# First FFN: block outputs stored by block, gathered by token in the attention stage; block list from six batches

## The chip, the core and the metric

The kernel runs on one core of one Trainium2 chip. The metric is device time in microseconds (us) of one launch; below it is the median over several runs. Engines: PE (TensorE, matrix products), DVE (VectorE), ACT (ScalarE), POOL (GpSimd) and SP (SyncE, which here only starts plain DMAs). POOL starts the indirect DMAs, whose row numbers come from a table in SBUF.

## The reference

One macaron block on x of 8 batches x 1024 tokens x 256 features, in f32:

```python
x = x + 0.5 * ffn(layernorm(x))
x = x + linear_attention(layernorm(x))
x = x + 0.5 * ffn(layernorm(x))
```

`ffn` is a mixture of 16 experts with two chosen per token, plus a shared expert for every token:

```python
weights, idx = gate(xf)              # softmax scores, 2 of 4 groups kept, then the top 2 experts
combine = (one_hot(idx, E) * weights[..., None]).sum(1)
h = silu(einsum(xf, We1) + be1) * (einsum(xf, We3) + be3)
y = einsum(combine, einsum(h, We2) + be2)
z = silu(xf @ ws1 + bs1) * (xf @ ws3 + bs3) @ ws2 + bs2
return y + z
```

The linear attention has 16 heads of 16 features: relu on queries and keys, a sum of keys and a context matrix per head over all 1024 tokens of a batch, a division by the key sum, and an output projection with bias.

## The kernel before

**Sizes.** T = 8192 tokens; a token's row has D = 256 floats. Rows are handled in blocks of RB = 256, on 128 partitions x 2. A batch is 8 tiles of 128 tokens. With two experts per token there are 16384 routed rows in each FFN.

**Four kinds of stage, in order.**

1. *Routing, 0 to about 250 us.* Round by round (`for r in range(B + 1)`), for each batch: layer norm and transposes (`normed`), the gate and the row numbers (`route`, a chain of small steps on PE and DVE), and the shared expert of an earlier batch (`shared_units`). `route` ends with 16 indirect DMAs on POOL per batch (L467) that scatter the batch's normalised rows to the table `xs_d`, sorted by expert. A row there is 264 floats: 256 of data, then the row number of the output and the gate weight, which an iota (L456) and a small product (L461) on POOL put there, for each of the two choices.
2. *Blocks of the first FFN, about 250 to 530 us.* A block is 256 rows of one expert ("whole"), or two half blocks of 128 rows of any experts ("pair"). Which rows a block takes is read from lists made on the chip. The list of whole blocks is made by `first_map` from the counts after seven of the eight batches, so that blocks can run while the last batch is routed: N1 = 40 whole blocks. The rest, N2 = 64 half blocks, is listed by `second_map` once all eight are counted. 69 blocks (`USUAL`) always run; three more stand under a condition and run only if the counts need them (here they don't).
3. *Linear attention, about 530 to 1004 us*, in 10 rounds: round r begins batch r (`begin`: take up the first FFN's outputs with `combine`, layer norm, transposes), runs the attention of batch r-1, and finishes batch r-2 (`finish`: layer norm and routing for the second FFN).
4. *Blocks of the second FFN* and a tail with the shared expert's units and the output, to the end.

**One block.** `rows` (L654 whole, L660 pair) loads the rows from `xs_d` into a buffer `xg` (4 buffers) through SP's queue. `weights` (L672) copies the expert's weights. `transpose` turns the rows on PE (L678, into `pxg`), ACT copies them out (L683, `xgT`), and DVE copies the two extra columns into `at` (L686, L687; 6 buffers). `first` is the first product on PE (L699), with silu on ACT (L705) and the gate product on DVE (L706, `hb`). `second` is the second product on PE (L725, `qy`); DVE adds the bias (a copy of which, `b2c`, L723, it made) and multiplies by the gate weight (L731, one instruction per 128 rows, `yo`), and POOL scatters each 128 rows by token to `ys_d` (L736), two indirect DMAs a block.

The order of the blocks' instructions is written by hand: in iteration i come the row load of block i+4, the weights of i+2, the transposes of i+1, the first product of i, the second product of i-2, and one step of the side work (`behind`: the last batch's routing, the second list, and DMAs that fill the ends of the experts' tables).

**Taking up the outputs.** In `combine`, SP loads a batch's two output rows per token from `ys_d` in eight plain DMAs of 256 KB (L855), and DVE adds each to x (L856, 128x512). In `attention`, DVE adds the projection's bias (L867, `bpj`); PE makes keys and queries (L877, `pk`) and their sums (L885, `pgs`); DVE makes `dg` (L896), from which PE spreads the key sums (L901); then come the context, the projection (L946, L954, `pp`) and the sum into x.

Each engine takes its instructions in the order of the program. In all stages but the blocks, a scheduler sets that order.

Of the kernel before, what the change touches and what calls it, by code (L numbers as in the profile page):

```python
# [11 lines left out]
I32 = mybir.dt.int32  # L12
# [14 lines left out]
def macaron_kernel(  # L27
# [36 lines left out]
    CAP = T + P  # L64
    DR = D + 8
    SKIP = 1 << 24
# [4 lines left out]
    N1 = ((T - N) * K - E * (RB - 1)) // RB // VL * VL  # L71

    N2 = -(-((K * T - E) // P + E - NR * N1) // VL) * VL
    NBLK = N1 + N2 // NR
    NBH = -(-max(N1, N2 + 1) // VL) * VL
# [20 lines left out]

    xs_d = tc.dram_tile([E * CAP + RB, DR], F32, name="xs_d")
    xs_views = dram_disjoint_views(xs_d, B * NT * K + E + 2)
# [70 lines left out]
    iblk = ramp(NBH, 0, 1, "iblk")  # L169
    gm1 = ramp(NG, -1, 1, "gm1")  # L170
# [6 lines left out]
    headmask = const.tile([P, P // HD, HD], F32, name="headmask")  # L177
# [136 lines left out]
    def route(base, which, b, xns, xnT, fine=False):  # L314

        name = f"{which}_{b}"

# [13 lines left out]
        for nb in range(NB):  # L331
# [25 lines left out]
        hi = rp.tile([P, npair], F32, tag="hi", name=f"hi_{name}")  # L357
        lo = rp.tile([P, npair], F32, tag="lo", name=f"lo_{name}")
        nc.vector.tensor_tensor(hi[:], pairs[:, :, 0], pairs[:, :, 1], ALU.max)
        nc.vector.tensor_tensor(lo[:], pairs[:, :, 0], pairs[:, :, 1], ALU.min)  # L360
# [3 lines left out]
        g2 = rp.tile([P, NT * NG], F32, tag="g2", name=f"g2_{name}")  # L364
        l2 = rp.tile([P, NT * NG], F32, tag="l2", name=f"l2_{name}")
        gsv = gs.rearrange("p j g -> p (j g)")
        nc.vector.tensor_tensor(l2[:], lv[:, :, 0], lv[:, :, 1], ALU.max)
        nc.vector.tensor_tensor(g2[:], hv[:, :, 0], hv[:, :, 1], ALU.min)
        nc.vector.tensor_tensor(g2[:], g2[:], l2[:], ALU.max)
        nc.vector.tensor_tensor(gsv, hv[:, :, 0], hv[:, :, 1], ALU.max)  # L370
        nc.vector.tensor_tensor(gsv, gsv, g2[:], ALU.add)
# [10 lines left out]
        won = rp.tile([P, NT, NG], F32, tag="won", name=f"won_{name}")  # L382
        lost = rp.tile([P, NT, NG], F32, tag="lost", name=f"lost_{name}")
        nc.vector.tensor_reduce(lost[:], cg.rearrange("p j a g -> p j g a"), axis=AX.X, op=ALU.add)
        nc.vector.tensor_reduce(won[:], cg[:], axis=AX.X, op=ALU.add)
        nc.vector.tensor_tensor(lost[:], lost[:], won[:], ALU.subtract)
        nc.vector.tensor_tensor(
            lost[:], lost[:], gm1[:].unsqueeze(1).to_broadcast([P, NT, NG]), ALU.is_ge
# [57 lines left out]
        row = rp.tile([P, NT, K], F32, tag="row", name=f"row_{name}")  # L446
        nc.vector.tensor_reduce(row[:], tmp[:], axis=AX.X, op=ALU.add)
        rowi = rp.tile([P, NT, K], I32, tag="rowi", name=f"rowi_{name}", bufs=2)
        nc.vector.tensor_copy(rowi[:], row[:])
# [30 lines left out]
    def counts(base, name, unit):  # L480

        cnt = rp.tile([1, E], F32, tag="cnt", name=f"cnt_{name}", bufs=2)
        nc.vector.tensor_tensor(cnt[:], base[0:1, :], eoff[0:1, :], ALU.subtract)
        nc.vector.tensor_scalar(cnt[:], cnt[:], 1.0 / unit, None, ALU.mult)
        return cnt

    def whole(cnt, name, op):

        more = half("xn", [1, E, MB], f"more_{name}")
        nc.vector.tensor_tensor(  # L490
            more[:], cnt[:].unsqueeze(2).to_broadcast([1, E, MB]),
            iblk[0:1, 0:MB].unsqueeze(1).to_broadcast([1, E, MB]), op,
        )
        nblk = rp.tile([1, E], F32, tag="nb", name=f"nb_{name}")
        nc.vector.tensor_reduce(nblk[:], more[:], axis=AX.X, op=ALU.add)
        return nblk

    def listed(nblk, off, name, res, unit):
# [35 lines left out]
        if off is not None:  # L534

            nc.vector.tensor_copy(rv[:, N2 : N2 + 1], end[:, E - 1 : E])
# [8 lines left out]
    def first_map(base, which):  # L545


        name = f"{which}a"
        cnt = counts(base, name, RB)
        nc.vector.tensor_scalar(cnt[:], cnt[:], -1.0, None, ALU.add)  # L550
        nblk = whole(cnt, name, ALU.is_ge)
        maps = []
        for _ in listed(nblk, None, name, maps, RB):
            pass
        end = rp.tile([1, E], F32, tag="done", name=f"done_{name}", bufs=2)
        nc.vector.tensor_tensor_scan(end[:], ones[0:1, 0:E], nblk[:], 0.0, ALU.mult, ALU.add)
        nc.vector.tensor_tensor(end[:], end[:], nblk[:], ALU.subtract)
        nc.vector.tensor_scalar(end[:], end[:], -1.0, float(N1), ALU.mult, ALU.add)
        nc.vector.tensor_scalar(end[:], end[:], 0.0, None, ALU.max)
        nc.vector.tensor_tensor(end[:], end[:], nblk[:], ALU.min)  # L560
        nc.vector.tensor_scalar(end[:], end[:], float(NR), None, ALU.mult)

        fill = half("xn", [P, DR], f"fill_{which}")
        nc.gpsimd.memset(fill[:], 0.0)
        nc.gpsimd.memset(fill[:, D : D + 1], float(SKIP))
        return maps, end, fill

    def second_map(base, which, maps, done):
# [7 lines left out]
        yield from listed(nblk, done, name, maps, P)  # L576

    def fill_up(last, fill):

        v = xs_views[B * NT * K + E]  # L580
        nc.sync.dma_start(out=v[E * CAP : E * CAP + P, :], in_=fill[:])
        for e in range(E):
# [11 lines left out]
    def behind(routing, base, which, maps, done, fill):  # L594

        for _ in range(7):
            next(routing)
            yield
# [3 lines left out]
        fills = fill_up(last, fill)  # L602
# [9 lines left out]
    def blocks(maps, which, steps, between, tail):  # L612
# [9 lines left out]
        b2 = biases(which)  # L622

# [25 lines left out]
        def rows(i):  # L649
            xg[i] = mid.tile([P, NR, DR], F32, tag="u1", name=f"xg_{which}_{i}", bufs=4)  # L650
# [23 lines left out]
        def transpose(i):  # L674
# [8 lines left out]
            nc.scalar.copy(xgT[i][:], pt[:])  # L683

# [26 lines left out]
        def second(i):  # L711
            py = ps_y.tile([P, NR, D], F32, tag="y", name=f"qy_{which}_{i}")
            yo = mid.tile([P, NR, D], F32, tag="u3", name=f"yo_{which}_{i}", bufs=4)
            h, a = hh.pop(i), at.pop(i)
            w2s = [wall[:, bass.ds(e, 1), W2 : W2 + D] for e in evals[i]]
            b2c = []
# [133 lines left out]
    def combine(which, b, xt):  # L850

        for j in range(0, NT, 2):
            for k in range(K):
                y = mid.tile([P, 2, D], F32, tag="u1", name=f"y_{which}_{b}_{j}_{k}", bufs=4)
                nc.sync.dma_start(out=y[:], in_=ys_v[k, b, :, j : j + 2, :])  # L855
                nc.vector.tensor_tensor(  # L856
                    xt[:, j : j + 2, :], xt[:, j : j + 2, :], y[:], ALU.add
                )
            yield
# [101 lines left out]
    def part(gen, n):  # L961

        for _ in range(n):
            next(gen, None)
            yield
# [11 lines left out]
    def normed(which, b):  # L977
# [3 lines left out]
        yield from layernorm(xs[b], f"f{which}_{b}", xns[b], DR, parts)  # L981
# [5 lines left out]
    for r in range(B + 1):  # L987
# [6 lines left out]
        if r >= 1:  # L994
            routing = route(base, 0, r - 1, xns.pop(r - 1), xnTs[r - 1], r == B)
        if r == B:
            maps, done, fill = first_map(base, 0)
            steps = behind(routing, base, 0, maps, done, fill)
        if r == B - 1:
            run(routing)  # L1000
        run(
            normed(0, r) if r < B else None,
            routing if r < B else part(routing, 2),
# [43 lines left out]
    def begin(b):  # L1047
        yield from combine(0, b, xs[b])
# [67 lines left out]
    def first_half():  # L1116
# [10 lines left out]
        maps, 1, behind(routing, base, 1, maps, done, fill), by_block(moves), first_half  # L1127
# [136 lines left out]
```

## Time and profile before

| | us |
|---|---|
| median of 6 runs (1388.65 to 1399.74) | 1391.33 |
| the profiled execution | 1383.5 |
| its span | 1381.8 |
| first block's transposes of the first FFN | 250.15 |
| its last block matmul ends | 521.46 |
| first load of block outputs | 530.14 |
| `dg` of batch 0 | 581.89 |
| first block of the second FFN | 1004.8 |
| tail | 1266 to 1381.8 |

The times in a trace are microseconds from the start of the span. The clock is the share of full speed that TensorE was granted, 0.941 in the mean. A line of a window gives the busy time (and instruction count) of PE, PE's weight loads, DVE, ACT and POOL in it, then the granted clock, the DMA engines' busy share, and GB/s. A line of a timeline gives start, duration, engine, line, operation and operands, shapes and count, and in brackets the idle time ahead with what ended it. `A <- B: 64.4, 24, 5.9` among the waits says that A waited for B for 64.4 us in all, 24 times, 5.9 us at most.

### The profile page before, as it was taken

Reading aid. Unit: us, or ns where it says so; the run is one execution under the profiler, and the core shown is the slowest. Engines: PE = TensorE matmul, PEld = TensorE weight load, DVE = VectorE, ACT = ScalarE, POOL = GpSimd, SP = SyncE. Lnnn points to the kernel's source line nnn. Section 1 sums busy time; section 2 is a strip of 40 time slices with the busy share of each in tenths; the row PEclk is TensorE's granted clock in tenths of the full one; section 3 lists DMA queues with packets and bytes.
Section 4 is the critical chain, followed back from the end, with each engine's and each line's share of the span. In section 5 each row is a group of like instructions: output and inputs, shape, how many; then the busy total and the mean of one; then the engine's idle time right before and its main releaser. Section 6 shows DMA issues by size and latency. Waiting matters only on the chain. (4 is left out here: it accounts for less than half of the span.)

```text
span 1381.8 us, 20671 instructions
## 1 busy us (share of the span) xinstructions
PE 1190.5 (86%) x5728; PEld 852.9 (62%) x5728; DVE 883.9 (64%) x2878; ACT 541.0 (39%) x1120; POOL 581.5 (42%) x719
## 2 busy tenths in 40 slices
PE   7898877688789997899878879899997889899997
PEld 3455444576678884566545546555576678786554
DVE  6786547566456566768648548637686545565587
ACT  6555422222225451554544544542432223453110
POOL 1566556265565552002252252350536666565010
PEclk9999999899899999999889889999998899999999
DMA  9334323455565534622362330110435555552996
GB/s 358 133 124 151 121 102 109 156 178 187 179 187 165 163 122 146 217 106 106 126 207 93 131 124 24 41 63 1 155 113 175 175 175 180 151 169 88 324 370 249
DMA packets 96102, 212.20 MB, mean 154 GB/s; under 512 B 17382, under 2 KB 45291, under 8 KB 92273
## 3 DMA queue, kind: packets, MB, share of 16 engines
q1 hardware_dynamic: 68288, 134.77, 30.4%
q0 software_dynamic: 27696, 76.07, 14.9%
q8 instruction: 49, 0.80, 0.3%
q14 instruction: 69, 0.56, 0.1%
HBM read 110.75 MB, written 102.64 MB: 154 GB/s over the span
## 5 line engine op out<-in xcount | busy, mean ns | idle before, releaser
L736 POOL DMA_INDIRECT ys_d<-yo,at x276 | 276.4, 1001 | 239.0 <-DVE rest L731 173.9
L699 PE MATMUL q<-xgT,wc 128*128 128x128 f32 (+1 forms) x1568 | 290.2, 335 | 60.1 <-ACT xgT L683 32.4
L467 POOL DMA_INDIRECT xs_d<-xn_f,rowi x256 | 263.9, 1031 | 111.3 <-issue 61.1
L699 PEld LDWEIGHTS q<-xgT,wc 128*128 128x128 f32 x1568 | 236.3, 199 | 88.3 <-ACT xgT L683 41.0
L683 ACT COPY xgT<-pxg 128x512 f32<-128x512 f32 x138 | 81.4, 590 | 281.9 <-PE pxg L678 94.1
L796 PE MATMUL p_s<-xnT_f,ws_sb 128*128 128x512 f32 x352 | 163.7, 604 | 1.1 <-ACT hs_s L800 0.9
L731 DVE CUSTOM_DVE_ANT_0 yo<-qy,b2c,at 128x256 f32<-128x256 f32 x276 | 122.8, 482 | 61.7 <-remote 19.1
L706 DVE SCALAR_TENSOR_TENSOR hb<-q,wc,hb 128x128 f32<-128x128 f32 (+1 forms) x196 | 73.5, 400 | 133.5 <-PE q L699 64.4
L815 PE MATMUL py_s<-ws_sb,hs_s 128*128 128x256 f32 x512 | 133.6, 405 | 29.1 <-DVE hs_s L801 21.9
L725 PE MATMUL qy<-wall,hb 128*128 x552 | 151.3, 398 | 3.3 <-DVE rest L731 2.5
L815 PEld LDWEIGHTS py_s<-ws_sb,hs_s 128*128 128x128 f32 x512 | 98.6, 200 | 66.0 <-DVE hs_s L801 34.1
L877 PE MATMUL pk<-wqk_sb,xnT_a 128*128 128x512 f32 x256 | 129.0, 623 | 0.2 <-ACT q L882 0.2
L461 POOL TENSOR_SCALAR xn_f<-cw 128x4 f32<-128x4 f32 x64 | 16.2, 259 | 251.2 <-DVE cw L433 248.3
L800 ACT ACTIVATE hs_s<-p_s,bc 128x512 f32<-128x512 f32 x64 | 43.8, 687 | 192.3 <-PE p_s L796 114.7
L725 PEld LDWEIGHTS qy<-wall,hb 128*128 128x128 f32 x552 | 106.2, 202 | 19.5 <-issue 5.2
L796 PEld LDWEIGHTS p_s<-xnT_f,ws_sb 128*128 128x128 f32 x352 | 66.5, 194 | 66.1 <-issue 61.3
L705 ACT ACTIVATE hb<-q,wc 128x128 f32<-128x128 f32 (+1 forms) x196 | 75.3, 419 | 73.8 <-PE q L699 37.8
L678 PE MATMUL pxg<-ident,xg 128*128 128x128 f32 x552 | 86.3, 282 | 9.2 <-DMA xg<-xs_d 9.2
L678 PEld LDWEIGHTS pxg<-ident,xg 128*128 128x128 f32 x552 | 72.3, 147 | 24.8 <-DMA xg<-xs_d 9.6
L801 DVE SCALAR_TENSOR_TENSOR hs_s<-p_s,bc,hs_s 128x512 f32<-128x512 f32 x64 | 47.6, 747 | 58.9 <-PE p_s L796 39.6
L885 PE MATMUL pgs<-xn_a,k 128*128 128x257 f32 x256 | 73.5, 405 | 10.8 <-issue 7.0
L796 PE MATMUL p_s<-xnTr,ws_sb 128*128 128x512 f32 x160 | 70.4, 593 | 0.3 <-PEq L786 0.3
(302 smaller groups left out, 1730.6 us busy)
## 6 DMA issues: line engine op xcount, KB each, us to landing
xg<-xs_d SPq DMA_DIRECT2D x80, 264.0 KB
y<-ys_d SPq DMA_DIRECT2D x64, 256.0 KB
y<-ys_d SPq DMA_DIRECT2D x32, 512.0 KB
xg<-xs_d SPq DMA_DIRECT2D x116, 132.0 KB
xk<-x SPq DMA_DIRECT2D x8, 1024.0 KB
x<-xk SPq DMA_DIRECT2D x8, 1024.0 KB
wall<-in_wexp_dram SPq DMA_DIRECT2D x4, 1540.0 KB
x<-in_x_dram SPq DMA_DIRECT2D x6, 1024.0 KB
```

Of the source, the lines that this page charges most:

```text
L467: nc.gpsimd.indirect_dma_start(out=v[:, :], out_offset=bass.IndirectOffsetOnAxis(ap=rowi[:, j, k : k + 1], axis=0), in_=xn[:, t, :], in_of ...
L678: nc.tensor.transpose(pt[:, c, s * P : (s + 1) * P], xg[i][:, s, c * P : (c + 1) * P], ident[:],)
L683: nc.scalar.copy(xgT[i][:], pt[:])
L699: nc.tensor.matmul(pt_[:, cs], w[:, s, o + c * P : o + (c + 1) * P], t[:, c, cs], start=(c == 0), stop=(c == NC - 1),)
L705: nc.scalar.activation(h[:, cs], p1[:, cs], AF.Silu, bias=w[:, s, W2 - 2 : W2 - 1])
L706: nc.vector.scalar_tensor_tensor(h[:, cs], p3[:, cs], w[:, s, W2 - 1 : W2], h[:, cs], ALU.add, ALU.mult)
L725: nc.tensor.matmul(py[:, s : s + 1, :], h[:, s * P : (s + 1) * P], w2s[s % len(w2s)], start=True, stop=True,)
L731: nc.vector.tensor_tensor_reduce(out=yo[:, s, :], in0=py[:, s, :], in1=b2c[s % len(w2s)][:, 0, :], scale=a[:, s, 1:2], scalar=0.0, op0=ALU ...
L736: nc.gpsimd.indirect_dma_start(out=ys_views[i * NR + s][:, :], out_offset=bass.IndirectOffsetOnAxis(ap=a[:, s, 0:1].bitcast(I32), axis=0), ...
L796: nc.tensor.matmul(pt[:], w[:, c, s * P : (s + 1) * P], xnT[:, c, :], start=(c == 0), stop=(c == NC - 1),)
L815: nc.tensor.matmul(py[:, t - t0, :], hs[s][:, t * P : (t + 1) * P], ws2_sb[:, s, :], start=(s == 0), stop=(s == NS - 1),)
L877: nc.tensor.matmul(pk.rearrange("p k d -> p (k d)"), tile_of(axnT, c, j), wqk_sb[:, c, :], start=(c == 0), stop=(c == NC - 1),)
```

## The change

Only the first FFN (`which == 0`) is changed. Its block outputs go, unweighted, to a new table `yt_d` in the order of the blocks, by one plain DMA per block. The attention stage fetches each token's two rows from there with indirect DMAs on POOL and multiplies by the gate weight while it sums. For that, the row number of each token's copy in `xs_d` is kept in SBUF (`row_of`) and turned into a row number of `yt_d` by `output_rows`; the weights are kept in `weight_of`. Rows in the first FFN's table have 256 floats and carry neither number nor weight.

The list of whole blocks is made from six batches: 32 whole blocks and 80 half blocks in the lists. 69 blocks still run, 32 whole and 37 pairs. The rows of the last two batches are scattered as side work of the block stage.

```diff
+    WIDTH = (D, DR)
...
-    N1 = ((T - N) * K - E * (RB - 1)) // RB // VL * VL
-
-    N2 = -(-((K * T - E) // P + E - NR * N1) // VL) * VL
-    NBLK = N1 + N2 // NR
+    LISTED = (B - 2, B - 1)
+    N1S = [(b * N * K - E * (RB - 1)) // RB // VL * VL for b in LISTED]
+
+    N2S = [-(-((K * T - E) // P + E - NR * n) // VL) * VL for n in N1S]
+    NBLK = max(n1 + n2 // NR for n1, n2 in zip(N1S, N2S))
...
+    yt_d = tc.dram_tile([NBLK * RB, D], F32, name="yt_d")
...
     (in route)
+        if which == 0:
+            nc.gpsimd.tensor_scalar(weight_of[:, b, :, :], cw[:], 0.5, None, ALU.mult)
+            yield
+            for k in range(K):
+                for j in range(NT):
+                    v = xs_views[(b * NT + j) * K + k]
+                    nc.gpsimd.indirect_dma_start(
+                        out=v[:, :],
+                        out_offset=bass.IndirectOffsetOnAxis(
+                            ap=rowi[:, j, k : k + 1], axis=0
+                        ),
+                        in_=xns[j // HT][:, j % HT, :], in_offset=None,
+                    )
+                    if fine or j % HT == HT - 1:
+                        yield
+            return
...
+    def output_rows(done):
...
+        for b in range(B):
+            row = row_of[:, b, :, :].rearrange("p j k -> p (j k)")
+            past = half("xn", [P, n, 2 * E], f"past_{b}")
+            nc.vector.tensor_tensor(
+                past[:], row.unsqueeze(2).to_broadcast([P, n, 2 * E]), flat(at), ALU.is_ge
+            )
+            nc.vector.tensor_tensor(past[:], past[:], flat(by_), ALU.mult)
+            move = rp.tile([P, n], F32, tag="row", name=f"move_{b}")
+            nc.vector.tensor_reduce(move[:], past[:], axis=AX.X, op=ALU.add)
+            nc.vector.tensor_tensor(row.bitcast(I32), move[:], row, ALU.add)
+            yield
...
     (in fill_up)
+        if which == 0:
+            n = (NBLK - USUAL) * NR
+            nc.sync.dma_start(
+                out=yt_d[USUAL * RB :, :].rearrange("(n p) d -> p n d", p=P),
+                in_=fill[:].unsqueeze(1).to_broadcast([P, n, D]),
+            )
...
-    def behind(routing, base, which, maps, done, fill):
-
+    def by(gen, lead, n):
+
+        for _ in range(lead):
+            next(gen)
+            yield
+        live = True
+        while live:
+            for _ in range(n):
+                live = next(gen, StopIteration) is not StopIteration
+            if live:
+                yield
+
+    def behind(routed, routing, base, which, maps, done, fill):
+
+
+        if routed is not None:
+            for _ in routed:
+                pass
+            yield
+            routing = by(routing, 7, HT)
...
     (in transpose)
             nc.scalar.copy(xgT[i][:], pt[:])
+            if which == 0:
+                xg.pop(i)
+                return
...
     (in second)
+            if which == 0:
+                for s in range(NR):
+                    nc.tensor.matmul(
+                        py[:, s : s + 1, :], h[:, s * P : (s + 1) * P], w2s[s % len(w2s)],
+                        start=True, stop=True,
+                    )
+                n = NR // len(w2s)
+                for s, e in enumerate(evals[i]):
+                    ss = slice(s * n, (s + 1) * n)
+                    b2e = b2[:, bass.ds(e, 1), :]
+                    nc.vector.tensor_tensor(
+                        yo[:, ss, :], py[:, ss, :],
+                        b2e if n == 1 else b2e.to_broadcast([P, n, D]), ALU.add,
+                    )
+                rows_ = "(p s) d -> p s d" if n > 1 else "(s p) d -> p s d"
+                nc.sync.dma_start(
+                    out=yt_d[i * RB : (i + 1) * RB, :].rearrange(rows_, s=NR), in_=yo[:]
+                )
+                return
...
-    def combine(which, b, xt):
-
-        for j in range(0, NT, 2):
+    def combine(b, xt):
+
+        for j in range(NT):
+            y = mid.tile([P, K, D], F32, tag="u1", name=f"y_0_{b}_{j}", bufs=4)
             for k in range(K):
-                y = mid.tile([P, 2, D], F32, tag="u1", name=f"y_{which}_{b}_{j}_{k}", bufs=4)
-                nc.sync.dma_start(out=y[:], in_=ys_v[k, b, :, j : j + 2, :])
-                nc.vector.tensor_tensor(
-                    xt[:, j : j + 2, :], xt[:, j : j + 2, :], y[:], ALU.add
+                nc.gpsimd.indirect_dma_start(
+                    out=y[:, k, :], out_offset=None, in_=yt_d[:, :],
+                    in_offset=bass.IndirectOffsetOnAxis(
+                        ap=row_of[:, b, j, k : k + 1].bitcast(I32), axis=0
+                    ),
+                )
+            for k in range(K):
+                nc.vector.scalar_tensor_tensor(
+                    xt[:, j, :], y[:, k, :], weight_of[:, b, j, k : k + 1], xt[:, j, :],
+                    ALU.mult, ALU.add,
                 )
             yield
...
-            routing = route(base, 0, r - 1, xns.pop(r - 1), xnTs[r - 1], r == B)
+            routing = route(base, 0, r - 1, xns.pop(r - 1), xnTs[r - 1], r > LISTED[0])
+        if r == LISTED[0]:
+            run(routing)
+            maps, done, fill = first_map(base, 0)
+        if r == B - 1:
+            routed, routing = routing, part(routing, 8)
         if r == B:
-            maps, done, fill = first_map(base, 0)
-            steps = behind(routing, base, 0, maps, done, fill)
-        if r == B - 1:
-            run(routing)
+            steps = behind(routed, routing, base, 0, maps, done, fill)
+            routing = part(routing, 2)
```

Beside this, the lists' helper tiles lie on all 128 partitions instead of one (the same number of elements per partition), `first_map` and `second_map` keep two offset rows per expert (`away`) for `output_rows`, and some temporaries of `route` and the head mask are made smaller.

## The prediction

> **What bounds the kernel now.** I read the page first, then windows, the DMA queue's waits, and the order of single instructions where the waits pointed.
>
> ```profile
> span 1381.8 us, 20671 instructions
> PE 1190.5 (86%) x5728; PEld 852.9 (62%) x5728; DVE 883.9 (64%) x2878; ACT 541.0 (39%) x1120; POOL 581.5 (42%) x719
> ...
> L736 POOL DMA_INDIRECT ys_d<-yo,at x276 | 276.4, 1001 | 239.0 <-DVE rest L731 173.9
> ...
> L467 POOL DMA_INDIRECT xs_d<-xn_f,rowi x256 | 263.9, 1031 | 111.3 <-issue 61.1
> ```
>
> PE is the busiest engine, and POOL's work is almost wholly indirect DMAs of about 1.0 us each. The span's chain of waits reaches back only over the tail, so stages must be read one by one.
>
> ```profile
> 240.00:260.00 20.00, 10.79 (x45) 8.86 (x44) 6.56 (x27) 3.77 (x7) 4.31 (x7) 0.74 0.59 200
> 340.00:360.00 20.00, 15.53 (x68) 12.92 (x67) 9.07 (x38) 3.38 (x7) 13.60 (x16) 0.83 0.66 217
> 480.00:500.00 20.00, 17.95 (x136) 16.43 (x135) 11.33 (x53) 9.75 (x26) 11.20 (x12) 1.00 0.53 153
> 600.00:620.00 20.00, 19.94 (x80) 11.64 (x78) 7.87 (x29) 14.77 (x37) 0.00 (x0) 1.00 0.41 149
> ```
>
> Windows: columns are PE, PE loads, DVE, ACT, POOL, granted clock, DMA share, GB/s. The first FFN's blocks (250 to 520) leave PE idle and at a clock of 0.83; the attention stage (600 to 620) fills PE with POOL empty. So the change takes work off POOL where PE waits and puts work on POOL where PE is the bound.
>
> ```profile
> SPq L654 <- DVE at L687: 64.4, 24, 5.9
> SPq L660 <- DVE at L687: 18.5, 9, 2.9
> SPq L654 <- DVE wc L672: 10.1, 4, 3.5
> SPq L654 <- DMA xs_d<-xn_f,rowi: 8.9, 3, 8.2
> SPq L660 <- DVE hb L706: 7.1, 3, 3.7
> SPq L654 <- PE pxg L678: 4.1, 4, 2.8
> ```
>
> The DMA queue's waits between 240 and 540 (us, times, longest): the load of a block's rows waits mostly for the `at` copies, which are the last readers of the row buffer four blocks earlier.
>
> ```profile
> 341.66 1.89 PE L699 MATMUL q<-xgT,wc 128*128 128x256 f32 x8
> ...
> 349.32 3.78 PE L699 MATMUL q<-xgT,wc 128*128 128x256 f32 x8 [4.47 <-issue]
> ```
>
> ```profile
> 343.46 1.00 POOL L736 DMA_INDIRECT ys_d<-yo,at  x1 [0.30 <-issue]
> 344.77 1.07 POOL L736 DMA_INDIRECT ys_d<-yo,at  x1 [0.30 <-issue]
> ```
>
> POOL issues one indirect DMA per about 1.28 us (1.0 plus 0.30), so a block's two scatters take 2.57 us of a block's 3.03 us; batch 7's routing scatters come on top. When POOL falls behind, `at` of block i waits for the scatter of block i-6 (six buffers), the row load waits for `at`, and PE waits for the rows: 4.47 us here, after which the same eight matmuls take 3.78 us instead of 1.89.
>
> **The change, part by part.**
>
> *Ahead of the blocks.* Block 0's rows now wait only for the scatters of batches 0 to 5; batch 6's 16 are issued after that. PE stood idle 9.21 us before its first block transposes at 250.15, for "DMA xg<-xs_d", while batch 6's scatters ran from 222.7 to 245.5. I take -9 us. Bounds: 0 (the routing chain of batch 6 is late instead) and -12 (the half-speed clock behind the gap, 0.74 in 240 to 260, goes too). The dropped iotas and small products (0.20 and 0.23 us) are off the path: 0, as POOL's end there no longer gates a block. Batch 5's routing, run to its end one round earlier, replaces the same serial run of batch 6: 0.
>
> *The blocks.* Gaps between the first transposes of neighbouring blocks sum to 159.0 us over 40 whole blocks and 102.7 us over 28 pairs; undisturbed ones are 3.03 and 3.09 us. Stalls are therefore 159.0 - 121.2 + 102.7 - 86.5 = 54.0 us. Of the row loads' waits inside the stage (the lines above without the one for xs_d: 104.2 us) `at` has 82.9, four fifths. The `at` copies are removed and the row buffer is freed by PE's transposes, so I credit 0.8 x 54 = -43 us. Eight blocks become pairs: 8 x 0.06 us, and many second pairs take 0.45 more: +2. DVE per whole block loses two `at` copies (0.33), a bias copy (0.28) and two products of 0.48 for one add of 128x512 (0.69, by L856's rows): -0.9 us x 69 = -60; the new map work adds 8 batches x 3 operations of 128x512, 8 x 2.1 = 17. Hidden, 0; without cover 0.25 us a block. SP's new store of 256 KB waits for DVE's add of block i-2, and the next row load is queued behind it. That load wants rows four blocks (12 us) ahead and took 2.2 us to land (345.61 to 347.80), so the wait hides; I put +1 for it. Batch 6's and 7's 32 scatters (41 us) now run on an otherwise empty POOL: 0. The second store of fill rows, 786 KB, goes beside DMA at 0.66 share: 0. Stage: -43 + 2 + 1 = -40. Bounds: -52 (all stalls gone), -10 (only the two longest PE gaps, 4.47 and 4.24 us, with their slow clock).
>
> *Handover.* PE's last block matmul ended at 521.46, but POOL scattered until 528.31 and the first load of results left at 530.14. Now an add (0.7) and the landing of a store (2.2) remain, then the same 1.8: about 526. I take -3; bounds 0 and -6.
>
> *The attention stage's start.* Call S the time of the first read of block outputs. Each batch needs 16 gathers on POOL in place of 8 loads on SP. In DVE's order all sums of batches 0 to 3 stand ahead of `dg` of batch 0, which gives PE its key sums. Before:
>
> ```profile
> 574.83 2.77 DVE L856 TENSOR_TENSOR x<-x,y 128x512 f32<-128x512 f32 x4 [1.21 <-DMA y<-ys_d]
> 579.08 0.69 DVE L856 TENSOR_TENSOR x<-x,y 128x512 f32<-128x512 f32 x1 [1.48 <-DMA y<-ys_d]
> 579.68 2.28 DVE L867 TENSOR_TENSOR xf<-xf,bpj 128x2048 f32<-128x2048 f32 x1
> 581.89 0.47 DVE L896 TENSOR_SCALAR dg<-ident,gk 128x128 f32<-128x128 f32 x2
> ```
>
> DVE's timeline shows batch 3's last adds directly ahead of `dg` at S + 51.8. No gather is in the trace; a scatter of the same 128 rows of 1 KB is nearest, so 64 x 1.28 = 82 us, and about 4.5 for the last landing and products: `dg` at S + 87, +35 us. PE's work ahead of it (keys and sums of batch 0) ended at S + 50 and ends some 9 us later, since batch 0's own sum is done at S + 24 instead of S + 15; PE then has nothing for about 28 us. It was at 19.94 of 20 us soon after, so the loss isn't won back. Bounds for a gather: 1.0 us (POOL's busy time alone), 64 + 4.5 = 68.5 or +17; 1.54 us (the slowest neighbours, 716.71 to 718.25), 103 or +51. The clock behind such a gap halves, as after 349.32: +2.
>
> The Trainium skill ("DMA: Bandwidth & Descriptors", section "Issuing engines are not separate DMA queues") says that choosing another engine to start DMAs saves only its issue time, usually small against the transfer. By that rule both moves, SP's stores and POOL's gathers, would be worth about nothing and the sum would be near the time before; the row of 1.28 us per indirect DMA on POOL speaks against it. The page "TensorE: Matmul & The Clock Gate", section "Part 1: The HAM clock gate", puts the clock at half after an idle window of some 3.4 us; by it one gap of 28 us costs one warm-up, no more than the +2 above.
>
> *Later rounds.* Of 53 us, POOL has 16 scatters (21.6 with their iotas), 16 gathers (20.5) and 2 of small work: 44 us. The gathers of the batch after next stand behind an iota that waits for PE (722.51) and ahead of the next scatters (751.11); eight end by about 733. DVE's sums cost 16 x 0.48 against 8 x 0.69, +2.2 us a batch, beside a DVE busy 7.87 of 20. I take 0; bounds -2 and +32 (8 us in each of four rounds).
>
> Sum: -9 - 40 - 3 + 35 + 2 = -15; I leave +2 for what a late gather does later: -13. The profiled run took 1383.5 us, 7.8 below the median of 1391.3; so 1370.5 on its basis, 1378 against the median.
>
> **The rivals.** B, slower: POOL becomes the bound of the attention stage beyond its start. In order, a gather that waits for a buffer or an iota holds up the scatters behind it and DVE's sums hold up `dg` in each round. For it: POOL's 44 of 53 us, in one queue; against: about 10 us of slack per round. At 8 us in four rounds, 1378 + 32 = 1410; it decides from 20 us on (1398). C: the block stage keeps its stalls because something else frees buffers or weights late (the waits for `wc` and `hb` above, or SP's store ahead of the row loads); the gain is 15 instead of 40: 1403. Against: `at` is named in four fifths. D: the start costs less because gathers run at 1.0 us or lose less: +17 instead of +35, 1360. Against: the 0.30 us pause stands in every pair of rows.
>
> **How the numbers follow.** A (forecast) 0.45, own range 1366 to 1392; B 0.27; C 0.12; D 0.16. About 0.5% (7 us) is what can be told from no change: faster is under 1384.4, slower over 1398.3. A gives 0.30, 0.12, 0.03 of faster, same, slower; B 0, 0.05, 0.22; C 0, 0.05, 0.07; D all faster. Together 0.46, 0.22, 0.32. The range goes from below D's 1360 to just past B's 1410: 1352 to 1412, leaving out the ends of both.
>
> **What will show it.** Row loads that no longer wait for DVE, transposes every 3.1 us, a stage from start to first read about 50 us shorter; then POOL in unbroken gathers for some 80 us, DVE waiting for `y`, and one long PE gap ahead of the key sums. Wrong it would be if block gaps stay near 4 us, if gathers are not about 1.3 us apart, or if rounds after 650 grow beyond 53 us.

## The result, and the profile after

The kernel after takes 1542.3 us (median of 20 runs, 1534.1 to 1551.4) against 1392.8 before (46 runs): a ratio of 1.109, 95% interval 1.106 to 1.111. It is slower by 150 us, far outside the range.

The head of the page after, and its costliest POOL groups (busy us, mean ns of one, then the idle time ahead):

```profile
span 1540.7 us, 20178 instructions
PE 1219.3 (79%) x5792; PEld 873.8 (57%) x5792; DVE 885.4 (57%) x2616; ACT 541.9 (35%) x1105; POOL 572.9 (37%) x652
...
L984 POOL DMA_INDIRECT y<-yt_d,row_of x128 | 141.0, 1102 | 307.6 <-PE p_s L925 162.1
L865 POOL DMA_INDIRECT ys_d<-yo,at x138 | 138.6, 1004 | 134.2 <-DVE rest L860 101.6
L472 POOL DMA_INDIRECT xs_d<-xn_f,rowi x128 | 132.9, 1038 | 77.1 <-issue 37.9
```

No engine is busier than before to speak of: PE has 29 us more, POOL 9 us less, and the span has 159 more. So some 130 of the 159 us are idle time of PE. Windows after (block stage, start of the attention, a later round):

```profile
400.00:420.00 20.00, 20.00 (x159) 19.00 (x157) 11.33 (x33) 11.14 (x25) 0.00 (x0) 1.00 0.73 230
...
590.00:610.00 20.00, 2.91 (x7) 1.85 (x6) 7.35 (x12) 0.66 (x2) 15.58 (x18) 0.58 0.32 92
...
700.00:720.00 20.00, 11.04 (x20) 5.55 (x21) 5.28 (x25) 5.70 (x13) 13.37 (x21) 0.73 0.38 140
```

Late in the block stage PE is full at full clock. At the start of the attention PE has 2.91 of 20 us while POOL gathers. But PE is half empty in a later round too. One window says little there, as PE's share swings within a round: before, it had 19.94 of 20 us from 600 to 620 and 12.81 from 700 to 720. Over all rounds behind `dg` of batch 0, PE was busy for 374 of 423 us before and for 409 of 531.5 after.

Chips differ here: the kernel before takes about 1372 to 1393 us on some chips (kind 1 below, that of the two profiles) and about 1240 on others (kind 2; the expectations call them slow and quick). A run is compared only with runs on its own kind, and both kernels were also run unchanged on one chip of kind 2. Terms of the span in us; "read" is the first read of block outputs, `dg` that of batch 0, and each column is one profile:

| | before, kind 1 | after, kind 1 | before, kind 2 | after, kind 2 | forecast |
|---|---|---|---|---|---|
| start to first block's transposes | 250.2 | 262.3 | 213.2 | 212.7 | -9 |
| first to last transposes | 262.0 | 240.1 | 220.4 | 213.4 | -40 |
| to the read | 17.9 | 11.6 | 15.3 | 11.7 | -3 |
| read to `dg` | 51.7 | 105.2 | 46.9 | 87.8 | +35 |
| `dg` to the second FFN | 422.9 | 531.5 | 402.5 | 484.0 | +2 |
| second FFN's transposes, tail | 376.9 | 389.9 | 339.6 | 341.6 | 0 |
| span | 1381.8 | 1540.7 | 1237.8 | 1351.1 | -15 |

On both kinds the largest term is the one forecast at nothing but 2 us for the clock behind the start's gap: the rounds after `dg` of batch 0, +108.6 and +81.5 us.

PE's waits of the kernel after on kind 1, from 505 to 1150, first in totals (us, times, longest) and then one place in PE's timeline ("issue" means that the profile shows nothing that the engine waited for):

```profile
PE pgs L1021 <- issue: 46.3, 12, 17.1
PE prk L429 <- DVE sel L419: 42.7, 6, 8.0
PE pgs L1021 <- ACT k L1017: 23.9, 6, 7.8
PE pm L1082 <- DVE cm L1078: 23.3, 7, 3.8
```

```profile
675.29 5.24 PE L1090 MATMUL pp<-mm,xnT_q 128*128 128x256 f32 x16
...
688.48 0.29 PE L429 MATMUL prk<-sel,nlow 128*128 128x128 bf16 x1 [7.95 <-DVE sel L419]
...
690.91 1.72 PE L294 MATMUL pt_a<-ident,xn_a 128*128 128x128 f32 x8
...
696.83 2.74 PE L1013 MATMUL pk<-wqk_sb,xnT_a 128*128 128x512 f32 x6
```

The same views of the kernel before (528 to 1005):

```profile
PE pgs L885 <- issue: 7.0, 4, 2.8
...
PE prk L416 <- DVE sel L406: 3.1, 5, 1.5
```

```profile
728.21 1.88 PE L877 MATMUL pk<-wqk_sb,xnT_a 128*128 128x512 f32 x4
...
735.14 3.19 PE L954 MATMUL pp<-mm,xnT_q 128*128 128x256 f32 x14
...
742.47 1.88 PE L877 MATMUL pk<-wqk_sb,xnT_a 128*128 128x512 f32 x4
...
747.71 0.22 PE L416 MATMUL prk<-sel,nlow 128*128 128x128 bf16 x1 [0.34 <-DVE sel L406]
```

`prk` is the product of the second FFN's routing that waits for a chain of DVE steps ending in `sel`. Before, keys of the next batch (`pk`) stand ahead of it and fill that wait, so 0.34 us is left. After, the transposes `pt_a` and keys `pk` come behind `prk`, and PE stands for 7.95 us with work in hand that needs none of it: ACT had written the last of the `xn_a` that `pt_a` turns by 661.6. One thing in the change bears on that order. The kernel's `run` takes one step of each generator of a round in turn, and a step of a generator ends at its `yield`. `combine` yields after each of 8 tiles, where it had yielded after each of 4 pairs, so the next batch has four more steps ahead of its PE work. The first experiments try that. (The first line of the totals, `pgs` with 46.3 us, is not of this kind: it is missing on kind 2, and part of it is taken up under the attention's start below.)

### The profile page after: what moved, and what is told of

Same layout as the page of the kernel before. It is cut to its first block, busy times and chain, and to the rows that moved or that the text cites. A ratio compares the mean times of both kernels' runs of the same rounds, so it can differ in the third digit from the quotient of the medians.

```text
span 1540.7 us, 20178 instructions
## 1 busy us (share of the span) xinstructions
PE 1219.3 (79%) x5792; PEld 873.8 (57%) x5792; DVE 885.4 (57%) x2616; ACT 541.9 (35%) x1105; POOL 572.9 (37%) x652
## 5 line engine op out<-in xcount | busy, mean ns | idle before, releaser
L808 PE MATMUL q<-xgT,wc 128*128 128x128 f32 (+1 forms) x1632 | 286.9, 327 | 58.5 <-ACT xgT L789 35.2
L808 PEld LDWEIGHTS q<-xgT,wc 128*128 128x128 f32 x1632 | 240.1, 200 | 80.8 <-ACT xgT L789 40.2
L984 POOL DMA_INDIRECT y<-yt_d,row_of x128 | 141.0, 1102 | 307.6 <-PE p_s L925 162.1
L865 POOL DMA_INDIRECT ys_d<-yo,at x138 | 138.6, 1004 | 134.2 <-DVE rest L860 101.6
L1021 PE MATMUL pgs<-xn_a,k 128*128 128x257 f32 x256 | 80.4, 442 | 70.6 <-issue 46.3
L1013 PE MATMUL pk<-wqk_sb,xnT_a 128*128 128x512 f32 x256 | 134.9, 653 | 0.0
L1021 PEld LDWEIGHTS pgs<-xn_a,k 128*128 128x128 f32 x256 | 49.6, 211 | 111.2 <-issue 62.6
L991 DVE SCALAR_TENSOR_TENSOR x<-y,weight_of,x 128x256 f32<-128x256 f32 x80 | 36.5, 478 | 81.5 <-DMA x<-xk 69.8
L1017 ACT ACTIVATE k<-pk 128x256 f32<-128x256 f32 x64 | 24.4, 382 | 164.4 <-remote 68.5
```

Of the source, the lines that this page charges most:

```text
L808: nc.tensor.matmul(pt_[:, cs], w[:, s, o + c * P : o + (c + 1) * P], t[:, c, cs], start=(c == 0), stop=(c == NC - 1),)
L865: nc.gpsimd.indirect_dma_start(out=ys_views[i * NR + s][:, :], out_offset=bass.IndirectOffsetOnAxis(ap=a[:, s, 0:1].bitcast(I32), axis=0), ...
L984: nc.gpsimd.indirect_dma_start(out=y[:, k, :], out_offset=None, in_=yt_d[:, :], in_offset=bass.IndirectOffsetOnAxis(ap=row_of[:, b, j, k : ...
L1013: nc.tensor.matmul(pk.rearrange("p k d -> p (k d)"), tile_of(axnT, c, j), wqk_sb[:, c, :], start=(c == 0), stop=(c == NC - 1),)
L1021: nc.tensor.matmul(pgs[c][:], kh[nb][:, t, c * P : (c + 1) * P], axn[nb][:, t, :], start=(j == 0), stop=(j == NT - 1),)
```

## The experiments

Where no repeats are given, a number is one run with a profile; before ran beside it.

### Which of the gathers and the eight steps costs the attention stage (kind 2)

Plain loads in place of the gathers, same bytes; this leaves out which rows a token takes:

```diff
-            for k in range(K):
-                nc.gpsimd.indirect_dma_start(out=y[:, k, :], in_=yt_d[:, :], ...
+            o = (b * NT + j) * K * P
+            nc.sync.dma_start(
+                out=y[:], in_=yt_d[o : o + K * P, :].rearrange("(p k) d -> p k d", k=K)
+            )
```

> The changed kernel with the attention stage's indirect gathers replaced by plain loads on SP: one DMA of 256 KB per tile of 128 tokens, eight per batch as before, from consecutive rows of yt_d. Which rows a token takes is left out; the products with the weights, their number and the eight steps per batch stay. Theory POOL (the gathers on POOL's in-order queue cost the 162 us that were lost between the first read and the second FFN): that stretch goes back from 637 to 475 +- 15 us and the whole to about 1380. Theory order (eight steps per batch and sixteen products in place of eight sums move the transposes and keys of the next batch behind the routing chain): the stretch stays above 570 us and the whole above 1470.

Four steps as before, gathers kept:

```diff
-            yield
+            if j % 2:
+                yield
```

> The changed kernel with the sum over outputs cut into four steps per batch, two tiles each, as before the change; gathers and products stay. Theory order: rounds after the first go back from about 70 to 53 us and the whole to about 1435. Theory POOL: within 10 us of 1540.

Both edits together (the same part left out as in the first), and both kernels unchanged on the chip of kind 2:

> Plain loads on SP (which rows a token takes is left out) and four steps per batch, both at once, to complete the square of gathers or not, four steps or eight. If the two losses are separate, the attention stage from the first read to the second FFN is as long as before's (within 12 us) and the whole is 0 to 25 us under before, by the block stage's gain. If the sixteen products of DVE in place of eight sums cost, the rounds stay above 53 us.

> The kernel before, unchanged, so that its stages can be read on the chip of these runs: on the chip of the first four runs it took 1242 us and not 1391. Every theory expects the time of before.

> The changed kernel, unchanged, on the same chip. If the losses found in its first profile (53 us at the attention stage's start, some 20 us a round after it) belong to the kernel, the round is 61 to 64 us where before has 50, and the whole stands about 8 to 11% over before. If they belong to the first chip, under 4%.

Measured, in us:

| kind 2 | whole time | before beside it | read to `dg` | `dg` to second FFN |
|---|---|---|---|---|
| before (8 plain loads, 4 steps) | 1239.5 | 1243.0 | 46.9 | 402.5 |
| plain loads, 4 steps | 1233.8 | 1243.0 | 53.1 | 400.8 |
| gathers, 4 steps | 1281.6 | 1242.3 | 87.7 | 411.3 |
| plain loads, 8 steps | 1312.1 | 1242.3 | 54.7 | 479.4 |
| gathers, 8 steps (after) | 1352.8 | 1243.0 | 87.8 | 484.0 |

The two parts are nearly independent, as far as one run of each shows. Eight steps cost 78.6 us (plain) and 72.7 (gathers) in the rounds and almost nothing at the start. Gathers cost 33.1 and 34.6 us at the start and 4.6 to 10.5 in the rounds. So POOL isn't the bound of the rounds: without a gather on it they still take 479.4.

PE's waits and the window of the rounds, gathers with eight steps:

```profile
PE prk L429 <- DVE sel L419: 42.7, 6, 7.9
PE pks L1037 <- DVE dg L1032: 23.1, 1, 23.1
PE pm L1082 <- DVE cm L1078: 22.1, 7, 3.6
PE pgs L1021 <- ACT k L1017: 16.5, 8, 5.5
```

```profile
525.00:1009.00 484.00, 391.28 (x1714) 258.35 (x1715) 280.40 (x804) 200.28 (x423) 201.16 (x245) 0.88 0.25 86
```

The same, gathers with four steps:

```profile
PE pks L1038 <- DVE dg L1033: 23.7, 3, 22.9
PE pt_a L294 <- ACT gsum L1050: 13.4, 5, 4.9
...
PE prk L429 <- DVE sel L419: 4.9, 5, 1.5
```

```profile
525.00:938.00 413.00, 370.94 (x1714) 246.21 (x1715) 278.17 (x804) 199.90 (x424) 209.20 (x246) 0.95 0.30 101
```

The 71 us between these windows divide so: PE's busy time for the same 1714 products falls by 20.3, as the granted clock rises from 0.88 to 0.95, and its idle time by 50.7 (92.7 to 42.1). The wait of `prk` gives 37.8 of it. The waits of `pm` and `pgs` shrink by some 22 and 14 us more, and those of `pt_a` and others take most of that back. The wait for `dg`, which the gathers cause, stays at 23 us.

On kind 1 the same edit was run beside the kernel after (before: 1391.5 us):

> The changed kernel once more, as the measure for the next two on their chip. Two of the chips so far took about 1240 us for the kernel before, two others 1372 and 1391. On one of the slow ones the stage from first to last transposes is 240 us, on a quick one 213.

> The changed kernel with four steps per batch, on the same chip. If the eight steps cost by the order of PE's work, the stretch from dg of batch 0 to the second FFN falls by 70 us or more on any chip; on a slow one the rounds with gathers and scatters together stay some us longer than before's.

After took 1531.2 us, with four steps 1461.7; the rounds fell from 534.8 to 460.1, by 75 us, and the start stayed at 106.6 and 105.1. With four steps the rounds are still 37 us above the profile of before; on kind 2 they are 9 us above it.

### Whether `dg` could go ahead of the later sums

Four steps, and an operation of DVE on the weights of batch b+2 (b+3 in the second kernel) that needs `gk`, put behind `dg`, so that DVE can't sum that batch ahead of `dg` of batch b; it leaves the values as they are:

```diff
+        if b + 2 < B:
+            w = weight_of[:, b + 2, :, :]
+            nc.vector.scalar_tensor_tensor(w, w, gk[:, 0, D : D + 1], w, ALU.min, ALU.max)
```

> Gathers, four steps per batch, and one small instruction of DVE after each batch's dg that rewrites the weights of the batch two later with themselves, so that the sums of batches 2 and 3 cannot stand ahead of dg of batch 0. If the start's loss comes from the 64 gathers ahead of dg, dg of batch 0 comes at 52 to 62 us after the first gather (about 92 with four steps alone), and the whole is 25 to 40 us under four steps alone. If POOL's rate bounds the stage anyway, the 30 us come back in the rounds behind it and the whole is within 10 us of four steps alone.

> As the order experiment before, with the small instruction after dg rewriting the weights of the batch three later: only batch 3's sums are kept behind dg of batch 0. If the gathers cost what POOL's queue needs in all, wherever it is paid (first gather to second FFN 497 to 499 us in both earlier cuts), dg of batch 0 comes at 72 to 78 us after the first gather and the sum is again 490 to 500. If there is slack between, the sum falls by 10 us or more.

On kind 2 the first took 1278.8 us against 1281.6 with four steps alone. `dg` came at S + 63.4 instead of 87.7, but read to second FFN took 497.3 us against 499.1: the rounds took back what the start gave. On kind 1 the second took 547.7 for that stretch, against 565.1 in the seven-batch kernel below, which has the same attention stage without the hold; so there 17 us were to be had, from one run each. Neither makes up for the gathers.

### Whether `at` stalled the block stage

The kernel before, with 8 buffers of `at` instead of 6, and with 16 (for which the head mask is made BF16, as in the change):

```diff
-            at[i] = mid.tile([P, NR, 2], F32, tag="at", name=f"at_{which}_{i}", bufs=6)
+            at[i] = mid.tile([P, NR, 2], F32, tag="at", name=f"at_{which}_{i}", bufs=8)
```

> The kernel before with eight instead of six buffers for the two extra columns (at), nothing else. If the wait of at for the scatter of six blocks earlier made the stalls, as the prediction had it, two more blocks of room shorten each FFN's block stage by 10 to 25 us and the whole by 20 to 50. If POOL's rate or the outputs' own four buffers bound it, the whole stays within 7 us of before.

> The kernel before with eight at buffers once more, timed in rounds. The first look was 0.6% under before. Theory at: 0.3 to 0.8% faster with an interval clear of 1. Rival: no difference that can be told.

> The kernel before with sixteen at buffers; the head mask is bf16 to make room for them. If at is still what row loads wait for with eight, another 2 to 5 us per FFN; if the four buffers of the outputs (yo, whose wait appears with eight) are the next bound, as with eight within 3 us.

One run on kind 2 took 1234.3 us against 1242.3. Repeated on kind 1 there is no gain: a ratio to before of 1.004 (1.001 to 1.007) with 8 buffers and 1.001 (0.998 to 1.004) with 16; first to last transposes took 255.3 and 259.5 us in the two profiles. With 16 buffers the row loads still wait 89 us for `at`, and the stage is still 52 us above its length without a stall (207.7 us, worked out below). The theory that the ring of `at` is what stalls the blocks falls. The DMA queue's waits of the kernel before on kind 2, over its block stage, show where the reading went wrong:

```profile
SPq L654 <- DVE at L687: 77.2, 34, 5.4
SPq L660 <- DVE at L687: 32.5, 27, 2.4
```

The queue waits 110 us for `at`, and yet the stage takes 220.4 us, only 13 more than the 40 x 3.03 + 28 x 3.09 = 207.7 us that it takes at the pace of its undisturbed blocks. This queue runs four blocks ahead, so it waits for buffers without a stall of PE. The list of PE's waits in the block stage of the kernel before on kind 1 has no wait for rows behind the first block; its largest lines, and the place of the 4.47 us that the prediction put down to the rows, are these:

```profile
PE q L699 <- ACT xgT L683: 19.1, 13, 4.2
PE q L699 <- issue: 12.4, 9, 4.5
```

```profile
344.26 0.60 PE L678 MATMUL pxg<-ident,xg 128*128 128x128 f32 x4
...
348.69 0.59 ACT L683 COPY xgT<-pxg 128x512 f32<-128x512 f32 x1 [8.39 <-remote]
```

"Remote" means that the trace names no instruction of the core as what ended the wait. The rows had come, and PE had turned them by 344.86; ACT, idle for 8.39 us, copied them only at 348.69, and the first product followed at 349.32. So what came late was ACT's copy.

### What did slow the blocks

Two indirect DMAs a block on POOL added to the kernel after. They write to tables that nothing reads (these and the row numbers are set up ahead, which the cut leaves out), take their data from the weights' tile, and nothing waits for them:

```diff
+                for s in range(NR if i < USUAL else 0):
+                    nc.gpsimd.indirect_dma_start(
+                        out=junk[i * NR + s][:, :],
+                        out_offset=bass.IndirectOffsetOnAxis(
+                            ap=idx[:, 0, 0:1].bitcast(I32), axis=0
+                        ),
+                        in_=wall[:, 0, 0:D], in_offset=None,
+                    )
```

> The changed kernel with two more indirect DMAs of POOL in each block of the first FFN, as many as before the change: each writes 128 rows of 1 KB from the weights' tile to a table of its own that nobody reads, and nothing waits for them. Theory signal (where POOL issues indirect DMAs the other engines' signals come late, on the slow chips): stalls of 2 to 10 us return in the blocks after the 19th and the stage grows by 10 to 25 us on a slow chip, not on a quick one. Theory wait (only what waits for POOL stalls, as the prediction had it): within 4 us of the changed kernel on any chip.

> The changed kernel with the two unused indirect DMAs of POOL per block once more, in the hope of a chip on which the kernel before takes about 1240 us. If the chip is a quick one: the stage from first to last transposes is 210 to 220 us, as without the extra DMAs. If it is a slow one: about 400 us again.

On kind 1 first to last transposes went from 236.5 to 408.6 us; on kind 2, from 213.4 to 215.5. The kernel with the added DMAs on kind 1, timelines of PE, ACT and POOL:

```profile
349.81 0.60 PE L790 MATMUL pxg<-ident,xg 128*128 128x128 f32 x4
...
379.19 3.78 PE L814 MATMUL q<-xgT,wc 128*128 128x256 f32 x8 [28.78 <-ACT xgT L795]
```

```profile
344.91 0.59 ACT L795 COPY xgT<-pxg 128x512 f32<-128x512 f32 x1 [14.38 <-remote]
...
378.55 0.59 ACT L795 COPY xgT<-pxg 128x512 f32<-128x512 f32 x1 [25.48 <-remote]
```

```profile
354.18 0.97 POOL L850 DMA_INDIRECT junk<-wall,idx  x1 [0.30 <-issue]
355.45 0.97 POOL L850 DMA_INDIRECT junk<-wall,idx  x1 [0.30 <-issue]
```

PE's four transposes of a block are done at 350.4, and ACT's copy of them starts at 378.55, 28 us later. POOL, which waits for nothing here, runs ahead of the blocks and issues one DMA after the other, 112 in a row from 354.2 to 498.6; four blocks there take 34 to 45 us each, and behind them a block takes 3.0 to 3.1. The same on kind 2:

```profile
323.62 0.59 ACT L795 COPY xgT<-pxg 128x512 f32<-128x512 f32 x1 [1.12 <-PE pxg L790]
326.70 0.59 ACT L795 COPY xgT<-pxg 128x512 f32<-128x512 f32 x1 [1.12 <-PE pxg L790]
```

There each copy starts 1.12 us after ACT's work before it, beside the same train of DMAs on POOL. So on kind 1 an unbroken train of indirect DMAs on POOL makes other engines start late, without any wait for them in the program.

The block stages of the other profiles agree. Before, POOL scattered through all of it, and long gaps stand in all of it on kind 1; ACT's "remote" waits there come to 46 us, and on kind 2 there are none. After, POOL scatters batch 6's rows from 262.9 to 283.1 and batch 7's from 305.2 to 327.2. Beside or just behind these stand the longest blocks, the 6th with 14.22 us and the 14th and 15th with 8.50 and 10.13; on kind 2 these three take 3.03 beside the same scatters. From the 19th block on no block exceeds 3.1 us in either profile after. That the whole 54 us of before come from this is not shown by a run of its own.

The store of the blocks on POOL's queue instead of SP's (kind 2):

```diff
-                nc.sync.dma_start(
+                nc.gpsimd.dma_start(
                     out=yt_d[i * RB : (i + 1) * RB, :].rearrange(rows_, s=NR), in_=yo[:]
```

> The changed kernel with the block outputs' plain stores started by POOL instead of SP. Theory store (in the first 18 blocks of the first FFN a store waits on SP for DVE, which is busy with routing and lists, and the next row loads stand behind it): the stage from first to last transposes goes from 240 to about 215 us and the whole down by 20 to 25. Rival (DVE's side work holds up the gate product and the weights, so PE waits whatever SP does): the stage stays within 6 us of 240.

The whole took 1342.8 us against 1352.8 after, and first to last transposes 208.2 us instead of 213.4. At the undisturbed pace 32 whole blocks and 36 pairs take 208.2 as well. So SP's store ahead of the row loads costs about 5 us on kind 2, nearly all of it in the 17th and 18th block (6.70 and 4.74 us; with the store on POOL 3.03 each).

### Whether the list from six batches pays (kind 1)

Four steps, and the list made from seven batches as before:

```diff
-    LISTED = (B - 2, B - 1)
+    LISTED = (B - 1, B - 1)
```

> Gathers, four steps per batch, and the list of whole blocks made from seven batches again (40 whole, 29 pairs), with batch 6's rows scattered before the blocks as before the change. If the list from six batches gains what PE waits for ahead of block 0, the first block's transposes come 5 to 12 us later here than with four steps alone (214 us on the chip of the earlier runs). If the routing of batch 6 sets the start in both, within 3 us. Fewer side steps of DVE in the first blocks: the stage from first to last transposes 0 to 5 us shorter than 213.

Beside the four-step kernel with the hold on batch b+3, which differs up to the attention only in this: the first block starts at 264.2 us with seven batches and 258.8 with six, but first to last transposes take 225.5 against 236.6. The list from six starts 5 us earlier and its stage is 11 longer, a net loss of about 6 in one run each. The 6th block, with no scatter of batch 6 beside it, takes 3.96 us with the list from seven and 15.15 with that from six.

No changed kernel that does the whole work beats the kernel before: the plain loads of 1233.8 us leave out which rows a token takes.

## Why the prediction was wrong

**The step that failed** is "Later rounds", taken at 0 with bounds of -2 and +32. It added up POOL's and DVE's work and the moment at which gathers begin, and found slack. It never asked what the longer chain of `combine` does to the order in which a scheduler lays PE's instructions, though the front of the document says that a scheduler sets it. Eight steps for four cost 73 to 79 us on kind 2 and 75 on kind 1: more than all gains forecast (52). Mending this alone isn't enough: with four steps the kernel is still 39 us above before on kind 2 (1281.6 against 1242.3) and 70 on kind 1 (1461.7 against 1391.5), because the start's cost came as forecast and the gains of 49 us ahead of and in the blocks didn't (7.5 on kind 2, 9.8 on kind 1); on kind 1 the 37 us left in the rounds come on top.

**Attention start, +35 (+2 for the clock):** on kind 2 mechanism confirmed and size right. `dg` came at S + 87.8, forecast S + 87. The gathers alone cost 33 to 35; with the sums' new form the start lost 40.9. PE's gap was 23.1 us, forecast 28. (The start of before was 5 us shorter on kind 2 than on kind 1, hence a loss above 35.) PE's timeline after on kind 2, then DVE's:

```profile
501.27 1.13 PE L1021 MATMUL pgs<-xn_a,k 128*128 128x257 f32 x4 [0.47 <-ACT k L1017]
...
525.86 0.79 PE L1037 MATMUL pks<-dg,ones 128*128 128x128 f32 x2 [23.10 <-DVE dg L1032]
```

```profile
518.45 0.48 DVE L991 SCALAR_TENSOR_TENSOR x<-y,weight_of,x 128x256 f32<-128x256 f32 x1 [0.74 <-DMA y<-yt_d,row_of]
519.69 0.49 DVE L991 SCALAR_TENSOR_TENSOR x<-y,weight_of,x 128x256 f32<-128x256 f32 x1 [0.76 <-DMA y<-yt_d,row_of]
...
525.13 0.48 DVE L991 SCALAR_TENSOR_TENSOR x<-y,weight_of,x 128x256 f32<-128x256 f32 x1 [1.96 <-DMA y<-yt_d,row_of]
525.53 0.48 DVE L1032 TENSOR_SCALAR dg<-ident,gk 128x128 f32<-128x128 f32 x2
```

DVE adds one row set per gather, 1.24 us apart, each after a wait for `y`, and comes to `dg` only behind the last. On kind 1 the term is +53.5, just past the bound of +51, and its last part has another cause. The gathers' distances there are mostly 1.26 us too, and DVE's last sum ends at 605.3, S + 91. PE's and DVE's timelines:

```profile
607.78 2.08 PE L1021 MATMUL pgs<-xn_a,k 128*128 128x257 f32 x4 [17.09 <-issue]
```

```profile
604.86 0.48 DVE L991 SCALAR_TENSOR_TENSOR x<-y,weight_of,x 128x256 f32<-128x256 f32 x1 [1.93 <-DMA y<-yt_d,row_of]
619.28 0.28 DVE L1032 TENSOR_SCALAR dg<-ident,gk 128x128 f32<-128x128 f32 x1 [13.93 <-ACT gk L1028]
```

DVE is through with the sums and waits 13.93 us more for the key sums `gk`, since PE's `pgs` are late: ACT copied keys that PE had ready at 590.7 only at 607.34, beside POOL's row of gathers. That is the lateness of "What did slow the blocks", and the prediction had no term for it.

The Trainium skill ("DMA: Bandwidth & Descriptors", section "Issuing engines are not separate DMA queues"), weighed in the prediction, calls an engine's issue time usually small against the transfer. For these gathers the measurement decides against it: 64 of them on one engine cost the start 33 us (kind 2), and in the window from 590 to 610 (kind 1) POOL is busy for 15.58 of 20 us with the DMA engines at 0.32.

**Blocks, -40:** measured -21.9 on kind 1 and -7.0 on kind 2, and the reason given is wrong. The `at` copies were four fifths of the queue's waits but not of the stalls: more buffers for them gained nothing, and PE did not wait for rows behind the first block. The size of the stalls, 54 us on kind 1, was right (262.0 less 207.7). What the runs point to for the part that went is the empty POOL, not the freed buffer; 32 us are left (240.1 less 208.2), in the part where batches 6 and 7 are still scattered. "Batch 6's and 7's 32 scatters now run on an otherwise empty POOL: 0" is thus wrong on kind 1. SP's store was put at +1 and costs about 5 on kind 2. The clock of 0.83 that the prediction gives to this stage was that of one window of 20 us; others in it had up to 1.00.

**Ahead of the blocks, -9:** measured +12.1 on kind 1 and -0.5 on kind 2. On kind 2 PE's gap ahead of block 0 did shrink, but the first block came no earlier. Before, then after:

```profile
213.23 1.97 PE L678 MATMUL pxg<-ident,xg 128*128 128x128 f32 x8 [16.10 <-DMA xg<-xs_d]
```

```profile
181.88 0.69 PE L344 MATMUL pg<-ident,gT 128*128 128x128 f32 x2 [8.46 <-ACT gT L340]
...
212.66 1.94 PE L784 MATMUL pxg<-ident,xg 128*128 128x128 f32 x8 [5.75 <-DMA xg<-xs_d]
```

10 us of the gap went, and a wait of 8.46 us stands in the routing instead: "replaces the same serial run of batch 6: 0" was too simple. Kind 1's +12.1 isn't settled. First blocks there started at 250.2, 241.3 and 248.1 us in three profiles of before and its variants, and at 257.3 to 262.3 in the profiles with the list from six. Ahead of the first block PE's gap for the rows shrank only from 9.2 to 6.3 us, and its waits in the shared expert (`py_s`) grew from 21.5 to 34.1; why, no run shows.

**Handover, -3:** -6.3 on kind 1, just past the bound of -6, and -3.6 on kind 2.

**The rivals.** B had the right sign and the right place, rounds beyond the start, but not the mechanism: with no gather on POOL the rounds still lose 77 us (479.4 against 402.5). C had something: the store's 5 us, and a gain of 22 on kind 1 where it said 15; but most of the stalls that stayed there stand beside POOL's scatters, where the same blocks on kind 2 have none, and not behind a buffer or a weight. D fell: the gathers of the start came 1.25 us apart or more, not 1.0.

## What to carry to other kernels

Where a scheduler interleaves generators, the number of steps a generator yields is part of the program: when an edit changes it, compare the order on the bounding engine and see which filler work now stands behind a waiting instruction. A DMA queue's wait for a buffer is a stall only if the engine behind it idles; compare the stage with its unstalled length first, and read what the idle engine itself waited for. Work moved from a plain queue to indirect DMAs on POOL cost that engine 1.26 us for 128 rows here, and what stands behind the last of a series in another engine's order pays for the whole series.

## What the runs showed of the hardware

Two kinds of chip ran the same program at 1372 to 1393 us and at about 1240 us. No chip showed both; whether that lies in the chip itself or in some lasting state of it, no run shows. On the first, 138 indirect DMAs on POOL that nothing waits for lengthened a stage by 172 us (236.5 to 408.6), where one copy on ACT began 28 us after its input was done; on the second by 2 (213.4 to 215.5). Idle time that ends "remote" stands in every trace of kind 1, 137 to 259 us over all engines and 507 in the kernel with the added DMAs, most of it ACT's and DVE's; none of the nine traces of kind 2 has any. Which resource is held, and why chips differ, the traces don't show. The same lateness may be what is left of kind 1's rounds with four steps (37 us against 9): ACT's "remote" waits in them come to 44 us, and on kind 2 there are none. That wasn't tried by itself.
